# A four-layer transformer block on one core: the first norm and the last norm, taken tile by tile and moved to another engine

## The chip, the cores and the metric

The kernel runs on 1 core of one Trainium2 chip, in float32. The metric is the device time in microseconds; the median of three runs of the kernel before is 620.03 us (619.95 to 620.16). The core has five engines that run their own instruction streams in order: TensorE (PE in the profile, its weight loads PEld), VectorE (DVE), ScalarE (ACT), GpSimd (POOL) and SyncE (SP), which here only issues transfers.

## The reference, cut to what matters

```
x = h                                               # (2, 512, 256)
x = x + LN(attention(LN(x)))      # inside: its own LN with gain and bias, q/k/v for 16 heads of 128,
                                  # rotary embedding, causal softmax, output product, + its input
x = x + LN(ffn_nvfp4(LN(x)))      # gate, up, gelu, down; weights dequantised from 4-bit codes, 2048 wide
x = x + LN(linear_attention(LN(x)))   # running sums of k and k*v, q*kv / (q*k + eps), output product
x = x + LN(ffn_lut(LN(x)))        # gate, up, silu, down; weights looked up in a table of 16, 688 wide
```

LN takes mean and variance of each row of 256 and has no gain or bias of its own. The sums run in the order given, for 2 sequences of 512 rows.

## The kernel before

The 1024 rows are 8 tiles of 128 rows. A sequence has NT = 4 tiles; a unit is HT = 2 tiles (256 rows), and there are NUNIT = 4 units. Products need the contracted dimension on the partitions, so every normed tile is turned ("T" in a name: xT0 is the turned input of q, k and v, xT3 that of the last ffn).

The order of work is written out by hand. `slot(i)` (L1104) is one of the 32 heads: the scores of head i, the projections of q and k for head i + 1, the output product of head i - 2, the product of softmax and v of head i - 1, and the values of a later group of heads. pT, the softmax turned by VectorE and four transfers through SP, comes back one slot later. Pieces of work that wait for something (the norms, the linear attention, the last output) are generators, "chains"; PE's loops call `poll()` (L252), which resumes a chain when its planned time has come. The plan uses the estimated costs of `Engine.cost` (L111) and `Times`; only the order comes from it, and on the chip semaphores decide. Loads go through SP in program order.

The places that the change touches:

- **Start** (L297 to L301, L534 to L550): SP issues the four tiles of x, the columns of gains and biases, then wq, sin, wk, cos, the second halves of sin and cos, wv and so on. Nine warm-up matmuls (L554) run on PE on a tile of ones.
- **First norm** (`first_norms`, L580; its branch without wait from L685): for each of four tiles VectorE takes statistics and POOL takes a power for the factor rstd. For tiles 0 and 1 ACT writes mean - x into n (reading with a stride, `spread`, L627), then writes two diagonals -rstd, and PE multiplies n with the diagonal, which turns and scales in one product (L711). For tiles 2 and 3 VectorE writes (x - mean) * rstd and PE transposes (L725). ACT then applies gain and bias from PSUM to xT0, two tiles (256 columns) at a time (`affine`, L649). POOL and ACT copy xT0 into xTv, reordered for the values.
- **First q and k** (`projection`, L840): for head 0 in two halves of 256 columns. The first halves are started at L1226 to L1244. From L1243 on `halved` makes `matmul` (L276) split its stationary operand into two of 64 columns.
- **Norms between layers** (`norms`, L357): two statistics, x += y * rstd, two more statistics, n by ACT, VectorE transposes 32x32 blocks and SP sends four transfers (`by_blocks`, L386). Only for the last unit's third norm, PE transposes (L402) and ACT copies from PSUM, and `halved` is set back (L400).
- **Linear attention** (L1279), its output product po (L1350) and the last ffn: `silu_hidden` (L1373) in steps of two chunks o, `silu_out` (L1411), which makes two tiles one after the other, each accumulating six chunks in one of the two PSUM banks of tag "o", and `written` (L1429), which adds and stores.

Of the kernel before, what the change touches and what calls it, by code (L numbers as in the profile page):

```python
# [19 lines left out]
P = 128  # L20
# [3 lines left out]
D = 256  # L24
# [18 lines left out]
SWAPPED = (1, 2)  # L43
WARM = 9
REST = INTER - (NO - 1) * P
# [145 lines left out]
def sandwich_kernel(  # L191
    ctx: ExitStack,
    tc: tile.TileContext,
    x: bass.AP,
    wq: bass.AP,
    wk: bass.AP,
# [98 lines left out]


    x0 = [const.tile([P, NT, D], F32, name=f"x0_{b}") for b in range(B)]  # L297
    cols_sb = const.tile([P, 3 * NH + 2 * NK], F32, name="cols_sb")
    for t in range(NT):
        sync.dma_start(out=x0[0][:, t, :], in_=x[0][t * P : (t + 1) * P, :])  # L300
    sync.dma_start(out=cols_sb, in_=cols)  # L301
# [32 lines left out]
    def chunk(t, kc):  # L334

        return t[:, :, kc].rearrange("p a j t -> p j a t")
# [16 lines left out]
    def add_scaled(x, y, rstd):  # L353

        vector.scalar_tensor_tensor(x, y, rstd, x, ALU.mult, ALU.add)

    def norms(u, y, stage, to, eps=EPS, strided=False):  # L357

        x = [xs[u][:, j, :] for j in range(HT)]
        first = [stats(t, eps) for t in y]
        second = []
        for j in range(HT):
            yield until(first[j][0])
            add_scaled(x[j], y[j], first[j][0])
            second.append(stats(x[j], EPS))
        n = acts.tile([P, HT, D], F32, tag="ln", name=f"ln{stage}_{u}")


        by_blocks = (u, stage) != (NUNIT - 1, 3)
        for j in range(HT):
            rstd, shift = second[j]
            yield until(rstd, shift)
            to_n, from_x = n[:, j, :], x[j]
            if not by_blocks:
                to_n = to_n.rearrange("p (k f c) -> p k f c", k=NK, c=4)
                from_x = from_x.rearrange(
                    "p (c f k) -> p k f c" if strided else "p (k c f) -> p k f c", k=NK, c=4
                )  # L380
            elif strided:
# [4 lines left out]
        if by_blocks:  # L386

            tr = acts.tile([P, 4, NK, HT, 32], F32, tag="ln", name=f"tr{stage}_{u}")
            for j in range(HT):
                vector.transpose(  # L390
                    tr[:, :, :, j, :], n[:, j, :].rearrange("p (k c f) -> p c k f", k=NK, c=4)
                )
            for a in range(4):
                sync.dma_start(
                    out=to[:, a].rearrange("p k j t -> p (k j t)"),
                    in_=tr[32 * a : 32 * a + 32].rearrange("f c k j t -> f c (k j t)"),
                )
        else:

            halved[0] = False  # L400
            pt = bank("t")
            for kc in range(NK):  # L402
                for j in range(HT):
                    transpose(
                        pt[:, kc * TU + j * P : kc * TU + (j + 1) * P],
                        n[:, j, kc * P : (kc + 1) * P],
                    )
            for kc in range(NK):
                scalar.copy(
                    to[:, :, kc].rearrange("p a j t -> p j a t"),  # L410
                    pt[:, kc * TU : (kc + 1) * TU].rearrange("p (j a t) -> p j a t", j=HT, a=4),
                )
# [97 lines left out]
    with ExitStack() as at:  # L510
# [23 lines left out]
        first, second = slice(0, TU), slice(TU, S)  # L534
        load("q", 0, 0)
        sync.dma_start(out=sin_sb[:, first], in_=sin[:, first])
        load("k", 0, 0)
        sync.dma_start(out=cos_sb[:, first], in_=cos[:, first])
        sync.dma_start(out=sin_sb[:, second], in_=sin[:, second])
        sync.dma_start(out=cos_sb[:, second], in_=cos[:, second])  # L540
        load("v", 0)
        load("q", 0, 1)
        load("k", 0, 1)
# [36 lines left out]
        def first_norms(b, wait):  # L580
# [104 lines left out]
            else:  # L685
# [5 lines left out]
                def diagonal(t):  # L691
# [5 lines left out]
                    )  # L697

                for t in range(NT):
                    statistics(t)  # L700
                    variance(t)
                    if t < HT:
                        scalar.activation(*spread(t), AF.Identity, bias=mv[:, t, 0:1], scale=-1.0)
                    factor(t)
                for t in range(HT):
                    diagonal(t)

                quarters = [[bank(tag) for _ in range(NK)] for tag in "ts"]
                for t in range(HT):
                    for kc in range(NK):  # L710
                        matmul(  # L711
                            quarters[0][kc][:, t * P : (t + 1) * P],
                            n[0][:, t, kc * P : (kc + 1) * P],
                            wu[:, 0, (t + 1) * P : (t + 2) * P],
                            True,
                            True,
                        )
                centred(2)
                centred(3)
                for j in range(2):  # L720
                    if j:
                        yield 0.0
                        for kc in range(NK):
                            for t in (HT, HT + 1):
                                turn(quarters[1][kc][:, t % HT * P : (t % HT + 1) * P], kc, t)  # L725
                    for kc in range(NK):
                        affine(
                            scalar,
                            xT0[b][:, kc, j * TU : (j + 1) * TU],
                            quarters[j][kc][:, :TU],  # L730
                            kc,
                        )
            for kc in range(NK):
# [5 lines left out]
                )  # L739
            yield 30.0  # L740
            while holder[0] is not None:
# [98 lines left out]
        def projection(kind, i, tag="mm"):  # L840
# [9 lines left out]
            lo, hi = slice(0, 64), slice(64, 128)  # L850

            for cs in [slice(0, TU), slice(TU, S)] if i == 0 else [slice(0, S)]:
                ps = bank(tag)
                for kc in range(NK):
                    matmul(
                        ps[:, cs],
                        w[:, hh, kc, :],
                        chunk(xT0[b], kc) if b else xT0[b][:, kc, cs],
                        kc == 0,
                        kc == NK - 1,  # L860
                    )
                yield
                def by_scalar():
# [3 lines left out]

                first_half = i == 0 and cs.start == 0
                if i and (kind == "k") == (i > 1):
# [356 lines left out]
        pair = projection("q", 0), projection("k", 0, "o")  # L1226
        next(pair[0])
        begin(first, next(first))
        for rows, cs, base in (
            (slice(0, P), slice(S - P, S), 0),  # L1230
# [12 lines left out]
        halved[0] = True  # L1243
        next(pair[1])  # L1244
        for step in (*pair, *pair, *pair):
# [33 lines left out]
    def linear_attention(u):  # L1279
# [63 lines left out]
        for ch in range(NK):  # L1343
            for t in range(HT):
# [3 lines left out]
                yield 0.3  # L1348
        yield until(lT)
        po = bank("t" if last else "o")  # L1350
# [11 lines left out]

        yield from norms(u, [po[:, j * D : (j + 1) * D] for j in range(HT)], 3, t, 16 * EPS)
        xT3[u] = t
# [46 lines left out]
    def silu_out(u):  # L1411
        for t in range(HT):
            po = bank("o")[:, :D]
            last = (u, t) == (NUNIT - 1, HT - 1)
            for cs in [slice(0, P), slice(P, D)] if last else [slice(0, D)]:
                for o in range(NO):
                    matmul(
                        po[:, cs],
                        hT2[u % 2][:, o, t * P : (t + 1) * P],
                        wd[:, o, cs],  # L1420
                        o == 0,
                        o == NO - 1,
                    )
                    if o % 2 and (o + 1 < NO or cs.stop < D):
                        yield
            begin(written(u, t, po))
            yield

# [52 lines left out]
def _layout(i):  # L1481
# [21 lines left out]
    def turned(w):  # L1503
        return w.reshape(4, 32, -1).transpose(1, 0, 2).reshape(w.shape)

    def by_half(s):
        return s.reshape(4, 2, -1).transpose(1, 0, 2).reshape(s.shape)
# [12 lines left out]
    named = {  # L1520
        "x": i[a0 + "h"],
        "wq": by_head_chunk(i[a0 + "wq"]),
        "wk": by_head_chunk(i[a0 + "wk"]),
# [43 lines left out]
```

## Time and profile before

| | |
|---|---|
| median of 3 runs | 620.03 us |
| profiled execution | 620.06 us |
| its span | 618.1 us |
| PE busy | 611.0 us, 99% of the span |
| VectorE busy | 483.3 us, 78% |
| ACT busy | 312.0 us, 50% |
| POOL busy | 275.9 us, 45% |

The span is what the profile covers; the profiled execution took 1.96 us more than it. A line of a timeline is: start in us, length, engine, line of the code, operation, output<-inputs, shapes, count, and in brackets the idle time of the engine before it and what ended it. L183, L281 and L288 are lines of helpers that record every operation, so the names of the tiles tell which it is. PE is shown with 128*128 or 128*64, the size of its stationary operand; a float32 matmul leaves two records. "ps_mm", "ps_o", "ps_s" and "ps_t" are PSUM banks by tag, two of each. Lines with SPq are the issue of a transfer, not the transfer.

### The profile page before, as it was taken

How to read it: one execution, taken by the hardware profiler on the slowest of the kernel's cores; microseconds unless marked ns; L12 is line 12 of the kernel's file. 1: busy time of each engine (PE TensorE's matmuls, PEld its weight loads, DVE VectorE, ACT ScalarE, POOL GpSimd, SP SyncE). 2: the span in 40 equal slices, each digit the busy share in tenths (PEclk: the TensorE clock that was granted, in tenths of full speed). 3: DMA queues.
4: the chain of work that ended last, by engine and by line, in shares of the span. 5: the costliest groups of instructions: out<-in, count | busy, mean ns of one | idle time of the engine just before them, and what ended most of it. 6: DMA issues, size and time to landing. Idle time of an engine off the chain costs nothing.

```text
span 618.1 us, 13150 instructions
## 1 busy us (share of the span) xinstructions
PE 611.0 (99%) x4876; PEld 397.7 (64%) x4876; DVE 483.3 (78%) x1159; ACT 312.0 (50%) x717; POOL 275.9 (45%) x353
## 2 busy tenths in 40 slices
PE   8999999999999999999999999999999999999996
PEld 6555655555555555656667788888666666666676
DVE  6989989887887999989899989779985463384853
ACT  5657776776666657667566741234123313425130
POOL 5355656454553575755667300440360160163341
PEclk9999999999999999999999999999999999999999
DMA  8467474755547547556543521310000001001000
GB/s 227 137 168 211 107 198 125 173 165 147 155 125 182 164 113 190 156 143 173 124 130 63 131 57 24 113 35 18 1 20 19 1 1 35 1 5 31 27 27 18
DMA packets 43599, 60.90 MB, mean 99 GB/s; under 512 B 5136, under 2 KB 31504, under 8 KB 43536
## 3 DMA queue, kind: packets, MB, share of 16 engines
q1 hardware_dynamic: 43536, 60.07, 37.5%
q8 instruction: 39, 0.64, 0.4%
q14 instruction: 24, 0.20, 0.1%
HBM read 28.33 MB, written 1.05 MB: 48 GB/s over the span
## 4 chain that ended last, share of the span: by engine, by line
PE 96%; DVE 2%; issue 1%; DMA 0%; POOL 0%; ACT 0%; POOLq 0%; DVEq 0%
PE ps_mm L281 39%; PE ps_o L281 22%; PE ps_s L281 21%; PE ps_t L281 14%; DVE rr L183 0%; DMA x<-in_x 0%; DVE turned L183 0%; DVE st L183 0%; DVE wu L183 0%; DVE xTv L183 0%; DVE xT L183 0%; DVE ra L183 0%; DVE hT L183 0%; POOLq L1563 0%; PE ps_t L288 0%
## 5 line engine op out<-in xcount | busy, mean ns | idle before, releaser
L183 DVE SCALAR_TENSOR_TENSOR rr<-ps_mm,cols_sb,sin_sb 64x512 f32<-64x512 f32 (+1 forms) x126 | 93.4, 741 | 3.7 <-PE ps_mm L281 0.8
L183 POOL TENSOR_TENSOR wg<-wg,scratch 128x752 f32<-128x752 f32 x30 | 53.8, 1794 | 91.0 <-DVE scratch L183 88.7
L281 PE MATMUL ps_mm<-xT,wg 128*64 128x256 f32 (+2 forms) x680 | 85.8, 379 | 0.0
L183 ACT ACTIVATE p<-p,mn 128x512 f32<-128x512 f32 (+3 forms) x128 | 70.3, 551 | 28.1 <-DVE mn L183 27.9
L281 PE MATMUL ps_s<-xT,wu 128*64 128x256 f32 (+1 forms) x652 | 82.0, 379 | 0.0
L281 PE MATMUL ps_o<-wd,hT 128*64 128x256 f32 (+2 forms) x676 | 78.3, 375 | 0.0
L281 PE MATMUL ps_t<-pT,v 128*64 128x256 f32 (+3 forms) x512 | 75.1, 433 | 0.0
L281 PEld LDWEIGHTS ps_mm<-xT,wg 128*64 128x64 f32 (+2 forms) x680 | 56.5, 139 | 19.1 <-ACT ge L183 0.3
L281 PEld LDWEIGHTS ps_o<-wd,hT 128*64 128x64 f32 (+1 forms) x676 | 55.5, 141 | 20.7
L183 ACT ACTIVATE p<-p,rs 128x512 f32<-128x512 f32 (+3 forms) x128 | 61.4, 551 | 11.4 <-DVE rs L183 9.8
L281 PEld LDWEIGHTS ps_s<-xT,wu 128*64 128x64 f32 (+1 forms) x652 | 54.4, 139 | 18.1 <-DVE hT L183 0.3
L281 PEld LDWEIGHTS ps_t<-pT,v 128*64 128x64 f32 x512 | 42.0, 137 | 34.8 <-issue 25.5
L281 PE MATMUL ps_o<-wo,oT 128*64 128x256 f32 x512 | 61.4, 379 | 0.0
L281 PE MATMUL ps_mm<-xT,wq 128*64 128x512 f32 (+2 forms) x252 | 59.4, 582 | 0.4 <-ACT xT L183 0.4
L281 PE MATMUL ps_mm<-xT,wk 128*64 128x512 f32 x248 | 59.1, 592 | 0.0
L281 PEld LDWEIGHTS ps_o<-wo,oT 128*64 128x64 f32 x512 | 42.5, 137 | 25.2 <-issue 15.1
L183 POOL TENSOR_TENSOR ra<-ra,cos_sb 128x512 f32<-128x512 f32 (+1 forms) x33 | 41.1, 1246 | 39.3 <-ACT ra L183 37.1
L281 PE MATMUL ps_s<-kT,qT 128*64 128x64 f32 (+5 forms) x384 | 57.4, 425 | 0.1
L183 DVE STREAM_TRANSPOSE turned<-p 128x512 f32<-128x512 f32 (+3 forms) x128 | 54.1, 479 | 2.1 <-DMA pT<-turned 0.6
L281 PE MATMUL ps_mm<-wv,xTv 128*64 128x256 f32 x464 | 55.6, 379 | 0.0
L183 DVE TENSOR_TENSOR hT<-ge,ps_s 128x512 f32<-128x512 f32 x32 | 21.8, 684 | 41.6 <-ACT ge L183 22.9
L281 PEld LDWEIGHTS ps_s<-kT,qT 128*64 128x64 f32 x384 | 34.3, 137 | 24.2 <-issue 7.5
(157 smaller groups left out, 933.6 us busy)
## 6 DMA issues: line engine op xcount, KB each, us to landing
pT<-turned SPq DMA_DIRECT2D x128, 208.0 KB, 3.9
wo<-in_wo SPq DMA_DIRECT2D x17, 256.0 KB, 4.1
wv<-in_wv SPq DMA_DIRECT2D x16, 256.0 KB, 4.0
wq<-in_wq SPq DMA_DIRECT2D x15, 256.0 KB, 4.4
wk<-in_wk SPq DMA_DIRECT2D x15, 256.0 KB, 4.0
xT<-tr SPq DMA_DIRECT2D x44, 64.0 KB, 2.1
pk_g<-in_gate_p SPq DMA_DIRECT2D x4, 256.0 KB, 4.3
sc_g<-in_gate_s SPq DMA_DIRECT2D x8, 128.0 KB, 4.1
```

What stands on the lines that cost most here:

```text
L183: return write(*args, **more)
L281: nc.tensor.matmul(out[part], lhsT=lhsT[:, part], rhs=rhs, start=start, stop=stop, **more)
```

## The change

At the start:

- the host hands in tiles 0 and 1 of the first sequence with their columns reordered (`x_turned`), so ACT reads them contiguously; the true rows are loaded into the same place later, 20 planned us after the norm;
- tiles 0 to 3 are centred, turned and given gain and bias one by one, each with its own affine of 128 columns; of tile 1 VectorE makes one of the two;
- the first half of q is made tile by tile, and the products of q and k stand between the turns of tiles 2 and 3;
- wk is loaded ahead of sin, and the first half of cos behind wv; there are eight warm-up matmuls instead of nine.

At the end, for the last unit:

- its third norm is done like the others (VectorE transposes, transfers), but VectorE makes n as well as the sum for rstd (`last_norms`); PE transposes nothing, and `halved` stays set;
- the output product of its linear attention is planned 0.8 us earlier;
- the output product of the unit before (`silu_out(2)`) accumulates four chunks of both tiles, then the last two of both.

In the instruction lists of the two programs, all engines have the same order between the start and the last unit, but for the two reloads on SP, which stand behind the transfers of the second head's pT and ahead of the next loads of wk, wv, wo and of the gate's codes and scales. At the end, PE has the eight halved matmuls of the linear attention's output product four instructions earlier; VectorE has the add x<-ps_o of unit 1's second output tile behind the last three hT products of unit 2, where it stood ahead of two of them; ACT has the two x<-x,shift ahead of the last two si.

```
-WARM = 9
+WARM = 8
...
+        src = x_turned if t < HT else x[0]
+        sync.dma_start(out=x0[0][:, t, :], in_=src[t * P : (t + 1) * P, :])
...
+    def last_norms(u, y, to, eps):
+        x = [xs[u][:, j, :] for j in range(HT)]
+        def factors(y, eps):
...
+            vector.bn_stats(st, y)
+            vector.bn_aggr(mv, st)
+            vector.tensor_scalar(ve, mv[:, 1:2], eps, None, ALU.add)
+            pool.tensor_tensor(rstd, ve, mhalf[:, :1], ALU.pow)
+            return mv, rstd
+        first = [factors(t, eps) for t in y]
+        second = []
+        for j in range(HT):
+            add_scaled(x[j], y[j], first[j][1])
+            second.append(factors(x[j], EPS))
+        yield 2.3
...
+        for j in range(HT):
+            mv, rstd = second[j]
+            vector.tensor_scalar(n[:, j, :], x[j], mv[:, 0:1], rstd, ALU.subtract, ALU.mult)
+            turned_about(tr, n, j)
+        brought(to, tr)
+        yield 1.0
+        for j in range(HT):
+            mv, rstd = first[j]
+            pool.tensor_scalar(shift, mv[:, 0:1], rstd, -1.0, ALU.mult, ALU.mult)
+            scalar.activation(x[j], x[j], AF.Identity, bias=shift)
+        yield until(to)
...
         load("q", 0, 0)
+        load("k", 0, 0)
         sync.dma_start(out=sin_sb[:, first], in_=sin[:, first])
-        load("k", 0, 0)
-        sync.dma_start(out=cos_sb[:, first], in_=cos[:, first])
         sync.dma_start(out=sin_sb[:, second], in_=sin[:, second])
         sync.dma_start(out=cos_sb[:, second], in_=cos[:, second])
         load("v", 0)
+        sync.dma_start(out=cos_sb[:, first], in_=cos[:, first])
...
+                def centred_rows(t):
+                    scalar.activation(
+                        n[0][:, t, :], x0[b][:, t, :], AF.Identity, bias=mv[:, t, 0:1], scale=-1.0
+                    )
                 for t in range(NT):
                     statistics(t)
                     variance(t)
-                    if t < HT:
-                        scalar.activation(*spread(t), AF.Identity, bias=mv[:, t, 0:1], scale=-1.0)
+                    if t == 0:
+                        centred_rows(0)
                     factor(t)
+                diagonal(0)
+                centred_rows(1)
+                diagonal(1)
+                def turned_to(engines, t, pts):
+                    for kc in range(NK):
+                        affine(engines[kc], xT0[b][:, kc, t * P : (t + 1) * P], pts[kc], kc)
+                firsts = []
+                for t, tag in ((0, "t"), (1, "s")):
+                    firsts.append([bank(tag)[:, :P] for _ in range(NK)])
...
                 centred(2)
+                turned_to([scalar, scalar], 0, firsts[0])
+                turned_to([vector, scalar], 1, firsts[1])
                 centred(3)
+                pts = [bank("t") for _ in range(NK)]
+                for t in (2, 3):
+                    yield 0.0
                     for kc in range(NK):
+                        turn(pts[kc][:, (t - 2) * P : (t - 1) * P], kc, t)
+                    turned_to([scalar, scalar], t, [p[:, (t - 2) * P : (t - 1) * P] for p in pts])
...
-            yield 30.0
+            yield 20.0
+            if b == 0:
+                for t in range(HT):
+                    sync.dma_start(out=x0[b][:, t, :], in_=x_rows[b][t * P : (t + 1) * P, :])
+            yield 10.0
...
+                first_half = i == 0 and cs.start == 0
+                tiles = [slice(0, P), slice(P, TU)] if first_half and kind == "q" else [cs]
+                for n, (ts, kc) in enumerate((ts, kc) for ts in tiles for kc in range(NK)):
...
+                    if first_half and (kind, n) in (("q", 1), ("k", 0)):
+                        yield
...
         next(pair[0])
+        next(first)
+        next(pair[0])
+        next(pair[1])
         begin(first, next(first))
+        next(pair[1])
...
-        yield until(lT)
+        yield until(lT) - 0.8 * last
...
+        if u == NUNIT - 2:
+            parts = [(t, slice(0, D), os) for os in (range(NO - 2), range(NO - 2, NO)) for t in range(HT)]
+        else:
+            parts = [(0, slice(0, D), range(NO))]
+            parts += [(1, cs, range(NO)) for cs in (halves if u == NUNIT - 1 else [slice(0, D)])]
+        po = {}
+        for n, (t, cs, os) in enumerate(parts):
+            if t not in po:
+                po[t] = bank("o")[:, :D]
...
+    def turned_columns(x):
+        return x.reshape(-1, NK, 4, 32).transpose(0, 1, 3, 2).reshape(x.shape)
```

`turned_about` and `brought` are the VectorE transpose and the four transfers that `norms` had in its by_blocks branch.

More of the change, by code (lines that the diff above doesn't have):

```diff
@@ L194, in sandwich_kernel @@
     x: bass.AP,
+    x_turned: bass.AP,
     wq: bass.AP,
@@ L294, in until @@
         return max(0.0, times.written(*aps) - now[0])
+    x_rows = x
     x0 = [const.tile([P, NT, D], F32, name=f"x0_{b}") for b in range(B)]
@@ L299, in sandwich_kernel @@
     for t in range(NT):
-        sync.dma_start(out=x0[0][:, t, :], in_=x[0][t * P : (t + 1) * P, :])
+        src = x_turned if t < HT else x[0]
+        sync.dma_start(out=x0[0][:, t, :], in_=src[t * P : (t + 1) * P, :])
     sync.dma_start(out=cols_sb, in_=cols)
@@ L355, in add_scaled, with turning, turned_about, brought @@
         vector.scalar_tensor_tensor(x, y, rstd, x, ALU.mult, ALU.add)
+    def turning(u, stage):
+        return acts.tile([P, 4, NK, HT, 32], F32, tag="ln", name=f"tr{stage}_{u}")
+    def turned_about(tr, n, j):
+        vector.transpose(tr[:, :, :, j, :], n[:, j, :].rearrange("p (k c f) -> p c k f", k=NK, c=4))
+    def brought(to, tr):
+        for a in range(4):
+            sync.dma_start(
+                out=to[:, a].rearrange("p k j t -> p (k j t)"),
+                in_=tr[32 * a : 32 * a + 32].rearrange("f c k j t -> f c (k j t)"),
+            )
+    def last_norms(u, y, to, eps):
+        x = [xs[u][:, j, :] for j in range(HT)]
+        def factors(y, eps):
+            st = small.tile([P, 6], F32, tag="st", name="st")
+            mv = small.tile([P, 2], F32, tag="mv", name="mv")
+            vector.bn_stats(st, y)
+            vector.bn_aggr(mv, st)
+            ve = small.tile([P, 1], F32, tag="ve", name="ve")
+            vector.tensor_scalar(ve, mv[:, 1:2], eps, None, ALU.add)
+            rstd = small.tile([P, 1], F32, tag="rstd", name="rstd")
+            pool.tensor_tensor(rstd, ve, mhalf[:, :1], ALU.pow)
[6 more added lines that the diff above has]
+        yield 2.3
+        n = acts.tile([P, HT, D], F32, tag="ln", name=f"n_{u}")
+        tr = turning(u, 3)
+        for j in range(HT):
[6 more added lines that the diff above has]
+            mv, rstd = first[j]
+            shift = small.tile([P, 1], F32, tag="shift", name="shift")
+            pool.tensor_scalar(shift, mv[:, 0:1], rstd, -1.0, ALU.mult, ALU.mult)
+            scalar.activation(x[j], x[j], AF.Identity, bias=shift)
+        yield until(to)
     def norms(u, y, stage, to, eps=EPS, strided=False):
@@ L368, in norms @@
         n = acts.tile([P, HT, D], F32, tag="ln", name=f"ln{stage}_{u}")
-        by_blocks = (u, stage) != (NUNIT - 1, 3)
         for j in range(HT):
@@ L375, in norms @@
             to_n, from_x = n[:, j, :], x[j]
[L376 to L381, printed above, removed]
+            if strided:
                 to_n = to_n.rearrange("p (k m) -> p k m", k=NK)
@@ L385, in norms @@
         yield until(n)
[L386 to L412, printed above, removed]
+        tr = turning(u, stage)
+        for j in range(HT):
+            turned_about(tr, n, j)
+        brought(to, tr)
         for j in range(HT):
@@ L697, in diagonal @@
                     )
+                def centred_rows(t):
+                    scalar.activation(
+                        n[0][:, t, :], x0[b][:, t, :], AF.Identity, bias=mv[:, t, 0:1], scale=-1.0
+                    )
                 for t in range(NT):
@@ L701, in first_norms @@
                     variance(t)
-                    if t < HT:
-                        scalar.activation(*spread(t), AF.Identity, bias=mv[:, t, 0:1], scale=-1.0)
+                    if t == 0:
+                        centred_rows(0)
                     factor(t)
[L705 to L709, printed above, removed]
+                diagonal(0)
[7 more added lines that the diff above has]
+                    firsts.append([bank(tag)[:, :P] for _ in range(NK)])
                     for kc in range(NK):
                         matmul(
-                            quarters[0][kc][:, t * P : (t + 1) * P],
+                            firsts[t][kc],
                             n[0][:, t, kc * P : (kc + 1) * P],
@@ L718, in first_norms @@
                 centred(2)
+                turned_to([scalar, scalar], 0, firsts[0])
+                turned_to([vector, scalar], 1, firsts[1])
                 centred(3)
[L720 to L725, printed above, removed]
-                    for kc in range(NK):
[L727 to L732, printed above, removed]
+                pts = [bank("t") for _ in range(NK)]
+                for t in (2, 3):
+                    yield 0.0
+                    for kc in range(NK):
+                        turn(pts[kc][:, (t - 2) * P : (t - 1) * P], kc, t)
+                    turned_to([scalar, scalar], t, [p[:, (t - 2) * P : (t - 1) * P] for p in pts])
             for kc in range(NK):
@@ L853, in projection @@
                 ps = bank(tag)
-                for kc in range(NK):
+                first_half = i == 0 and cs.start == 0
+                tiles = [slice(0, P), slice(P, TU)] if first_half and kind == "q" else [cs]
+                for n, (ts, kc) in enumerate((ts, kc) for ts in tiles for kc in range(NK)):
                     matmul(
-                        ps[:, cs],
+                        ps[:, ts],
                         w[:, hh, kc, :],
-                        chunk(xT0[b], kc) if b else xT0[b][:, kc, cs],
+                        chunk(xT0[b], kc) if b else xT0[b][:, kc, ts],
                         kc == 0,
@@ L865, in by_scalar @@
                     pool.tensor_mul(a[:, cs], a[:, cs], cos_sb[:, cs])
-                first_half = i == 0 and cs.start == 0
                 if i and (kind == "k") == (i > 1):
@@ L1243, in sandwich_kernel @@
         halved[0] = True
-        next(pair[1])
         for step in (*pair, *pair, *pair):
@@ L1361, in linear_attention @@
         t = gp.tile(TURNED, F32, tag="xT3", name=f"xT3_{u}", bufs=4)
-        yield from norms(u, [po[:, j * D : (j + 1) * D] for j in range(HT)], 3, t, 16 * EPS)
+        y = [po[:, j * D : (j + 1) * D] for j in range(HT)]
+        yield from last_norms(u, y, t, 16 * EPS) if last else norms(u, y, 3, t, 16 * EPS)
         xT3[u] = t
@@ L1411, in silu_out @@
     def silu_out(u):
[L1412 to L1427, printed above, removed]
+        halves = [slice(0, P), slice(P, D)]
+        if u == NUNIT - 2:
[7 more added lines that the diff above has]
+                po[t] = bank("o")[:, :D]
+            for o in os:
+                matmul(
+                    po[t][:, cs],
+                    hT2[u % 2][:, o, t * P : (t + 1) * P],
+                    wd[:, o, cs],
+                    o == 0,
+                    o == NO - 1,
+                )
+                if o % 2 and (o + 1 < NO or cs.stop < D):
+                    yield
+            if o == NO - 1 and cs.stop == D:
+                begin(written(u, t, po[t]))
+                yield
     def written(u, j, y):
@@ L1521, in _layout @@
         "x": i[a0 + "h"],
+        "x_turned": turned_columns(i[a0 + "h"][0, : HT * P]),
         "wq": by_head_chunk(i[a0 + "wq"]),
```

## The prediction

> **What bounds the kernel now.** I read the page's busy line, then the chain that ended last, then the chain in order of time around the two places that the change touches, then the timeline there for what runs beside.
>
> ```profile
> PE 611.0 (99%) x4876; PEld 397.7 (64%) x4876; DVE 483.3 (78%) x1159; ACT 312.0 (50%) x717; POOL 275.9 (45%) x353
> PE 96%; DVE 2%; issue 1%; DMA 0%; POOL 0%; ACT 0%; POOLq 0%; DVEq 0%
> ```
>
> TensorE (PE) is 96% of the chain. From 8.06 us to the last matmul the chain has no piece of another engine, so time is won only by starting that unbroken stretch earlier or by taking PE work out of it. The pieces in the head, and in the tail:
>
> ```profile
> 5.32 0.95 PE ps_t L281 x6
> 6.27 0.03 issue
> 6.29 0.57 ACT xT L183
> 6.87 0.04 issue
> 6.91 1.16 PE ps_mm L281 x4
> 8.06 0.44 PE ps_s L288 x4
> 8.50 1.01 PE ps_o L281 x8
> 9.52 0.86 PE ps_mm L281 x8
> ...
> 592.66 1.73 PE ps_o L281 x16
> 594.39 0.59 PE ps_t L288 x4
> 594.97 3.46 PE ps_o L281 x16
> ```
>
> Columns: start, length, what. In the head PE alternates with ACT until 6.91; from there it is packed: first half of q (ps_mm), turn of tiles 2 and 3 (ps_s L288), first half of k (ps_o), second half of q at 9.52. In the tail four transposes take 0.59 between two groups of the last-but-one output product. Full-width and halved matmuls cost the same: the 8 halved records at 591.80 take 0.86 us and the 4 full ones at 598.43 take 0.86. So leaving the tail halved (line 400 is gone) is free, and I cost it at 0 (bounds -0.1 and +0.1 for the last product with 128 columns, whose 24 full records go at 0.11 each).
>
> **The head.** The timeline's rows for ACT and for the wait behind the second tile:
>
> ```profile
> 3.51 1.47 ACT L183 ACTIVATE n<-x,mv 128x256 f32<-128x256 f32 x2 [1.09 <-DVE mv L183]
> 4.88 0.68 ACT L183 ACTIVATE wu<-wu,rstd 128x128 f32<-128x128 f32 x2
> 6.29 1.02 ACT L183 ACTIVATE xT<-ps_t,cols_sb 128x256 f32<-128x256 f32 x2 [0.73 <-PE ps_t L281]
> ```
>
> ACT centres both tiles, then builds both diagonals, then both 256-wide affines. Now it goes tile by tile. Working forward with these durations:
>
> 1. Centring reads contiguously (x is turned on the host). Strided it took 0.74; the contiguous 256-wide ACTIVATE (p<-p,rs) takes 0.49, with some 0.4 to the next start. It starts at 3.51 as before; rstd of tile 0 is ready at 3.75+0.56=4.31, so diagonal 0 runs 4.34 to 4.72 (0.38). Tile 1's centring follows at 4.63, its diagonal (rstd at 4.48+0.55=5.03) 5.07 to 5.45.
> 2. PE turns tile 0 from 4.78 (was 5.32). A first 128-column record ends 0.38 after its start, each further one 0.11 later: 5.26 for the first half of the columns, 5.49 for the second; tile 1 ends 5.99 and 6.22.
> 3. The affines are 128 wide: 0.56 less 0.13 (the step between 256 and 128 columns at about 1 ns each) is 0.43. ACT does tile 0 at 5.36 and 5.69 (ends 6.13). VectorE's piece of tile 1 stands between n(2), which ends at 5.80+0.53=6.33, and n(3) at 6.78, where VectorE waited 0.45 for POOL anyway; at 0.35 (the 256-wide one from PSUM takes 0.48) it ends at 6.70 and costs nothing there.
> 4. PE: q of tile 0 ends at 6.7, tile 2's transposes at 6.9, q of tile 1 waits for 6.70 and ends at 7.46, k's first half-product 7.89, tile 3's transposes 8.11, k's second 8.54.
> 5. ACT's affines of tile 3 run 8.04 to 8.47 and 8.37 to 8.80. So the second half of q starts at 8.52; its first pair is out at 8.95, where before it was 9.35+0.38=9.73. **PE's stretch starts 0.78 us earlier.**
>
> What is late next: the scores start at 14.52 now, so at 13.74. They need kT and qT. VectorE's chain from the second half of q to kT is 10.58 to 14.36, 3.78 us; from 9.64 it ends at 13.42. POOL's qT (12.30 to 13.56 now) follows xTv, the three mask selects and two multiplies, which start 0.4 earlier, and ends near 13.2. Both are covered, by 0.3 and 0.5; if that cover is gone the gain falls by the difference. Transfers: wk and sin change places, and the first cos goes behind wv. By the transfer view the early 128 KB loads land 2.1 (x) to 4.4 us (the second wk) after issue, wv after up to 5.1. wk, issued at 3.52 and 3.0 in flight before, is needed at 7.4; cos, issued at 5.89, lands by 10.3 at the latest and POOL wants it near 10.4. The values need wv near 10.1; issued at 5.42 (now 5.89) it lands by 10.5 at the latest, which would cost up to 0.4.
>
> Removing one of nine warm-up matmuls takes nothing off the path: the last one starts at 4.40, real work at 5.32. The two reloads of x's tiles, issued on SP behind the second head's pT, cost SP two issues of about 0.6 (the row of xT<-tr); behind them stand six loads and the next pT. SP stood idle from 40.1 to 42.45 there, so 1.2 fits; the bandwidth for 256 KB (about 0.9 us at 290 GB/s) could push a pT against its product. Bounds 0 to 0.3 lost; I take 0. From there the instruction lists of the two programs are the same up to the last unit, so the shift is carried to the tail. Head: 0.78, bounds 0.4 (wv late, or POOL and VectorE end last) and 1.1 (no restart cost at any of PE's new waits).
>
> The warm-up rows show records 0.213 apart (9 records starting 1.78, 2.13 us in all), and 0.11 apart at the end (6 starting 3.70, 0.97 in all): PE runs at half rate until about 3.8, 2.8 us after the first. [...]
>
> **The tail.** The transposes on PE go: 0.59. In their place VectorE makes n, transposes it and SP sends four transfers. Working on the clock of before: the output product of the linear attention moves ahead of four matmuls and ends 0.86 earlier, 584.89. VectorE: two statistics, two adds, two more statistics at 0.43+0.18+0.15 and 0.49 each, the first output tile's two operations and the second's statistics, then n twice (about 0.4) and two transposes (0.43): to about 591.95. Four issues of 0.6 and 2.1 to landing make 596.0; PE wants xT at 597.8. So the transfer is hidden, by 1.8.
>
> But a new wait replaces the transposes. The last-but-one output product now accumulates both tiles side by side, so its second tile needs the other ps_o bank 1.7 us after the first, at 594.2. That bank is freed by VectorE's add x<-ps_o of the unit before, which stood at 590.79 and now is queued behind n, the transposes and all three hT products. The last hT cannot be earlier:
>
> ```profile
> 590.79 0.48 DVE L183 SCALAR_TENSOR_TENSOR x<-ps_o,rstd,x 128x256 f32<-128x256 f32 x1
> 592.79 0.64 ACT L183 ACTIVATE si<-ps_mm 128x256 f32<-128x256 f32 x2
> 593.66 0.42 DVE L183 TENSOR_TENSOR hT<-si,ps_mm 48x256 f32<-48x256 f32 x1
> ```
>
> It waits for si, which waits for PE's matmul that ends at 592.65. ACT has the two x<-x,shift ahead of si now; their shifts stand on POOL behind the second output tile's ve, rstd and shift, which take 1.32 after its statistics (596.52 to 597.84 in a later row), so they come at 590.46+1.32+2x0.26=592.3. So si starts near 592.9, hT ends at 594.2, the add at 594.68. PE starts then, first pair out at 594.73+0.43=595.16; unhindered it would be 594.60. Stall 0.56 of the 0.59. At best (si at 592.74) the add ends at 594.53 and the stall is 0.4; with VectorE's chain 0.3 later it is 0.85. **Tail: -0.03, bounds -0.2 and +0.3.**
>
> **Sum.** 620.06 (profiled execution; span 618.1 and 1.96 around it) - 0.78 - 0.03 = 619.25. The median of before is 620.03, 0.03 lower, so 619.2.
>
> **Rivals.**
> - *More is won*, 618.6: PE restarts cost less than 0.1 each and the head gives 1.1 to 1.2, with the tail at its best end of 0.2. For it: the weight loads run ahead of the matmuls (PEld 64%). Against: n(2) at 6.33 and VectorE's piece at 6.70 are fixed by POOL's rstd.
> - *The head's gain is lost*, 620.0: wv lands late, qT or kT ends last, or a pT lands behind the reloads, and the tail stalls 0.85. For it: cover of only 0.3 to 0.5. Against: SP's idle time and the unchanged order.
> - *Slower*, 621.6: eight warm-ups leave PE at half rate when the real work starts at 4.8. Until the second half of q, 20 records of 128 columns and 4 of 256 (28 units) would cost 0.1 more each, 2.8, of which about 0.5 falls in waits: 619.25+2.3. It decides only if full rate is not there by about 4.8; before, it came near 3.8, inside the eight.
> - *The change does not do what it says*: the tail is that case in part, as its PE time is given back as a wait.
>
> **Numbers.** Within 0.2% (1.24 us, about what a measurement here can tell from no change) lies 618.79 to 621.27. Forecast 0.63, more won 0.17, gain lost 0.14, slower 0.06. So faster 0.17, same 0.77, slower 0.06. Range: head 0.4 to 1.1, middle 0 to 0.3 lost, tail +0.2 to -0.3: 618.7 to 620.3, drawn to 618.5 for part of the second case.
>
> **What would show it.** Right: PE's second half of q near 8.5, the scores near 13.7, no transposes at the tail, and a wait of PE on VectorE (x<-ps_o) of about half a microsecond before the second tile of the last-but-one output product. Wrong: warm-up records still 0.21 apart at their end, PE waiting on a transfer (wv, cos, xT), or no wait in the tail.

## The result and the profile after

The changed kernel takes 619.11 us by median (618.87 to 619.63, 18 runs), the kernel before beside it 620.16 us (619.91 to 620.95, 18 runs). The ratio is 0.9984, 95% interval 0.9977 to 0.999: 1.05 us less, 0.16%, which is inside the 0.2% that count as no change here. The profiled execution took 618.87 us with a span of 617.1 (before: 620.06 and 618.1).

The page's busy line and its shares of the chain, after:

```profile
PE 610.6 (99%) x4966; PEld 413.4 (67%) x4966; DVE 485.4 (79%) x1168; ACT 309.7 (50%) x716; POOL 276.2 (45%) x347
PE 95%; DVE 3%; issue 1%; DMA 0%; POOL 0%; ACT 0%; POOLq 0%; DVEq 0%; ACTq 0%
```

PE has 0.4 us less to do, and VectorE's share of the chain has risen from 2% to 3%. The chain in order of time shows where. In the head (columns: start, length, what):

```profile
4.86 0.80 PE ps_t L282 x4
5.66 0.64 PE ps_s L282 x4
6.30 0.52 PE ps_mm L282 x4
6.82 0.22 PE ps_t L289 x2
7.04 0.45 PE ps_mm L282 x4
...
8.59 1.07 PE ps_mm L282 x8
9.66 0.86 PE ps_o L282 x8
```

The reader is to see that the chain now stays on PE from 4.86 on until the tail, with no piece of ACT between its products (before, ACT's xT stood at 6.29 and PE was packed from 6.91). The second half of q, x8 at 8.59, is to be compared by the timeline's starts, 8.58 against 9.35: the chain's 9.52 of before is only where the piece ahead of it ends. In the tail, the end of the same chain:

```profile
593.28 0.49 DVE x L183
593.77 0.14 issue
593.91 3.67 PE ps_o L282 x32
597.58 0.86 PE ps_mm L282 x8
```

The four transposes are gone, and in their place the chain leaves PE: the second tile of the last-but-one output product waits until VectorE's add x frees its bank. The list of PE's waits names it, the only one besides the wait for the first memset:

```profile
PE ps_o L581 <- POOL mhalf L183: 1.0, 1, 1.0
PE ps_o L282 <- DVE x L183: 0.5, 1, 0.5
```

To compare executions whose first transfer lands at different moments, I measured stretches between starts of PE records (and of VectorE's first statistic) in all twelve profiles. Columns: A from the first statistic to the values (ps_t<-wv); B from the values to the first scores; C from the first product of pT and v to the twenty-first; D from the first hidden product of the last-but-one unit to that of the last unit, which holds the tail's change; then the median, and the ratio to before with its interval (before was run again beside each of them, with medians of 620.16 to 620.20).

| run | A | B | C | D | median us | ratio (95%) |
|---|---|---|---|---|---|---|
| before | 8.24 | 3.45 | 216.46 | 11.82 | 620.16 | |
| after | 7.46 | 3.56 | 216.18 | 11.91 | 619.11 | 0.9984 (0.9977 to 0.9990) |
| e1 head only | 7.46 | 3.57 | 216.43 | 11.82 | 619.32 | 0.9986 (0.9977 to 0.9995) |
| e2 tail only | 8.31 | 3.44 | 216.20 | 11.90 | 619.82 | 0.9996 (0.9987 to 1.0004) |
| e3 in turn | 7.46 | 3.56 | 216.19 | 11.22 | 618.34 | 0.9971 (0.9960 to 0.9983) |
| e4 add early | 7.46 | 3.55 | 216.34 | 11.22 | 618.38 | 0.9972 (0.9961 to 0.9983) |
| e5 nine warm-ups | 7.46 | 3.55 | 216.78 | 11.90 | 619.18 | 0.9982 (0.9973 to 0.9991) |
| e6 four warm-ups | 8.66 | 3.56 | 216.19 | 11.91 | 620.52 | 1.0006 (0.9997 to 1.0015) |
| e7 strided | 7.96 | 3.57 | 216.19 | 11.90 | 619.20 | 0.9985 (0.9976 to 0.9994) |
| e8 old order | 7.68 | 3.57 | 216.18 | 11.91 | 618.92 | 0.9981 (0.9972 to 0.9990) |
| e9 contiguous only | 8.21 | 3.44 | 216.27 | 11.83 | 619.89 | 0.9995 (0.9986 to 1.0004) |
| e10 strided, in turn | 7.60 | 3.55 | 216.19 | 11.23 | 618.31 | 0.9970 (0.9959 to 0.9981) |

### The profile page after: what moved, and what is told of

Read it like the earlier page. It is cut to its first block, busy times and chain, and to the rows that moved or that the text cites. A ratio compares the mean times of both kernels' runs of the same rounds, so it can differ in the third digit from the quotient of the medians.

```text
span 617.1 us, 13345 instructions
## 1 busy us (share of the span) xinstructions
PE 610.6 (99%) x4966; PEld 413.4 (67%) x4966; DVE 485.4 (79%) x1168; ACT 309.7 (50%) x716; POOL 276.2 (45%) x347
## 3 DMA queue, kind: packets, MB, share of 16 engines
HBM read 28.59 MB, written 1.05 MB: 48 GB/s over the span
## 4 chain that ended last, share of the span: by engine, by line
PE 95%; DVE 3%; issue 1%; DMA 0%; POOL 0%; ACT 0%; POOLq 0%; DVEq 0%; ACTq 0%
PE ps_mm L282 39%; PE ps_o L282 21%; PE ps_s L282 20%; PE ps_t L282 14%; DVE st L183 0%; DVE x L183 0%; DVE rr L183 0%; DMA x<-in_x_turned 0%; DVE hT L183 0%; DVE turned L183 0%; DVE mv L183 0%; DVE wu L183 0%; POOL rstd L183 0%; DVE xTv L183 0%; DVE xT L183 0%
## 5 line engine op out<-in xcount | busy, mean ns | idle before, releaser
L282 PE MATMUL ps_mm<-xT,wg 128*64 128x256 f32 x704 | 86.1, 379 | 0.0
L282 PE MATMUL ps_s<-xT,wu 128*64 128x256 f32 x672 | 82.2, 379 | 0.0
L282 PE MATMUL ps_o<-wd,hT 128*64 128x256 f32 (+1 forms) x728 | 78.3, 372 | 0.5 <-DVE x L183 0.5
L282 PEld LDWEIGHTS ps_o<-wd,hT 128*64 128x64 f32 x728 | 54.9, 137 | 22.1 <-issue 0.9
L282 PEld LDWEIGHTS ps_mm<-xT,wg 128*64 128x64 f32 x704 | 56.2, 137 | 19.5 <-ACT ge L183 0.3
L282 PEld LDWEIGHTS ps_t<-pT,v 128*64 128x64 f32 x512 | 47.3, 137 | 29.5 <-issue 21.0
L282 PEld LDWEIGHTS ps_s<-xT,wu 128*64 128x64 f32 x672 | 54.2, 137 | 18.4 <-DVE hT L183 0.3
L282 PEld LDWEIGHTS ps_o<-wo,oT 128*64 128x64 f32 x512 | 46.9, 137 | 20.7 <-issue 14.0
L282 PE MATMUL ps_s<-kT,qT 128*64 128x448 f32 (+5 forms) x384 | 57.4, 425 | 0.1
```

What stands on the lines that cost most here:

```text
L282: nc.tensor.matmul(out[part], lhsT=lhsT[:, part], rhs=rhs, start=start, stop=stop, **more)
```

## The experiments

**e1, the head alone.** Before, with the first norm, q and k, loads and warm-ups of the change, and the old norms, linear attention and last output product.

> The head of the change on the kernel before; the tail is the old one, with its four transposes. My theory (head 0.72 us won, as the traces of before and after show at the values, 11.24 against 10.52; middle nothing; tail about nothing): 0.7 us faster than before, 0.6 to 0.8 by medians, a span of 617.2 to 617.4, no wait of PE in the last unit. Rival A, that the tail was worth the 0.3 us by which the two profiled executions differ beyond the head (1.19 in all): 0.7 here too, but about 0.3 in e2. Rival B, that these 0.3 us were won in the middle by the head (the reloads, the transfers' new order): 1.0 us faster. Rival C, chance: in the profile of before one head's pT landed at 170.32, 5.8 us after its last issue, where most take 4.0 to 4.7, and PE waited 0.2 for it; then here too the middle shifts by at most that 0.2 in one head, differently from run to run.

Measured: 619.32 us, 0.85 less than before. A is 7.46, as in after, D is 11.82, as in before, and C is 216.43, as in before. So the 0.28 by which after's profile is shorter in C is not the head's doing: rival B falls. Rival C holds in kind, though the shift can be larger than its 0.2 (0.54 at one head in e5). The profiled execution of before shows the cause in one head, in the timeline's row of the weight loads (in brackets: idle time before, and what ended it):

```profile
170.36 0.20 PEld L281 LDWEIGHTS ps_t<-pT,v 128*64 128x64 f32 x4 [0.46 <-DMA pT<-turned]
```

The last packet of that pT landed at 170.32, 5.8 us after its last issue. Over the twelve profiles C is 216.18 to 216.20 in seven and longer by 0.08 to 0.60 in five (before, e1, e4, e5, e9). In before, e1 and e5 the step lies at this same head, the fourteenth, whose last pT lands 4.5 to 6.0 us after its issue in the twelve (4.5 is the median of all heads); in e4 it lies at the third, where no late transfer was looked for. In e5, whose C is the longest, PE's list of waits shows it:

```profile
PE ps_t L282 <- DMA pT<-turned: 0.3, 1, 0.3
```

So a late pT is an event of an execution, with the change and without it (e5 differs from after by one warm-up only). What makes this head's transfer late was not tried.

**e2, the tail alone.** Before, with the last unit's norms by VectorE, the earlier output product of the linear attention, the interleaved output product and the halved tail.

> The tail of the change on the kernel before (nine warm-ups, the old head). My theory: the transposes' 0.59 us are given back by the wait for the ps_o bank; in after, the shift against before goes from 0.98 us ahead of the last-but-one unit's hidden product to 0.87 behind its output product, so the tail loses 0.1 there and wins 0.05 to 0.15 at the end (halved last product). Time within 0.15 us of before. Rival A (the tail wins the 0.3 that the head does not explain): 0.3 us faster. A wait of PE on VectorE's x of 0.4 to 0.6 us ahead of the second tile of the last-but-one output product in either case. In the middle nothing that differs from before but a single late pT.

Measured: 619.82 us, ratio 0.9996 (0.9987 to 1.0004), so no difference is shown, and by the times alone rival A's 0.3 is not excluded either. The trace is sharper here: D goes from 11.82 to 11.90, 0.08 lost, with a wait of PE on x of 0.5, as in after. Rival A's 0.3 would have to be somewhere in the trace; the stretches behind D (to the last unit's output product 9.50 against 9.49, and from there to the last add 7.04 against 7.07) give back 0.02 in all. So the work of the tail is worth nothing. Behind the last add the span ends 3.10 us later against 3.29 in before; that is not the tail's work either, as the part on the tail below shows.

**e3, the last-but-one output product in turn.** After, with one condition changed, so that the two tiles are made one after the other again:

```
-        if u == NUNIT - 2:
+        if u < 0:
             parts = [(t, slice(0, D), os) for os in (range(NO - 2), range(NO - 2, NO)) for t in range(HT)]
```

> After, with the last-but-one unit's output product tile by tile again (all six chunks of one tile, then of the other). Then the second ps_o bank is needed 2.6 us after the first product starts instead of 1.73, that is at 594.1 by after's clock, and VectorE's add frees it at 593.76. My theory: the wait (0.67 us between PE's records at 593.24 and 593.91) goes whole and nothing takes its place, since the two last hT chunks (592.79 and 593.25) are wanted at 593.24 and 593.67: 0.6 to 0.7 us faster than after, about 1.7 us faster than before. Rival: PE then waits for hT (the order that the change gave up was bad for that reason): the fifth chunk's semaphore comes some 0.1 late, so only 0.4 to 0.5 is won. Second rival: the next unit's xT is then late: it lands near 595, wanted at 596.7: no.

Measured: 618.34 us, 0.77 less than after and 1.83 less than before. D is 11.22: 0.69 less than in after, 0.60 less than in before, which is the transposes' 0.59. The chain has PE alone again in that place:

```profile
590.82 0.86 PE ps_mm L282 x8
591.68 5.18 PE ps_o L282 x48
596.86 0.86 PE ps_mm L282 x8
```

All 48 records of both tiles run without a gap, where after had 3.67 us of them behind a wait. Neither hT nor xT takes the wait's place: xT's last transfer landed at 595.01, 1.7 us ahead of its first use.

**e4, the add moved up.** After, with the add of the second unit's second tile planned one unit of time earlier; on VectorE it then stands ahead of the last two hT products, and PE's order is that of after:

```
-            yield until(rstd, shift)
+            yield until(rstd, shift) - 1.0 * ((u, j) == (1, 1))
             add_scaled(x, y, rstd)
```

> After, with the add x<-ps_o of the second unit's second tile (and the shift behind it) moved on VectorE ahead of the last two hT products, into the 0.82 us in which VectorE waits for si. The order of PE is that of after. My theory (the wait is for the bank that this add frees): the bank is free at about 592.1, the wait goes whole: 0.6 to 0.7 us faster than after, the same as e3 within 0.1. Rival (the wait is for something else that comes at the same time, hT or si): the wait stays, as in after, or grows by the 0.5 by which the hT products are pushed back.

Measured: 618.38 us, D 11.22, both as e3. VectorE's timeline, where the add (ps_o,rstd,x) fills the time in which VectorE waited for ACT's si:

```profile
590.91 0.65 DVE L183 TENSOR_TENSOR hT<-si,ps_s 128x512 f32<-128x512 f32 x1
591.48 0.47 DVE L183 SCALAR_TENSOR_TENSOR x<-ps_o,rstd,x 128x256 f32<-128x256 f32 x1
592.05 0.35 DVE L183 TENSOR_SCALAR x<-x,shift 128x256 f32<-128x256 f32 x1
592.38 0.42 DVE L183 TENSOR_TENSOR hT<-si,ps_s 128x256 f32<-128x256 f32 x1
592.83 0.42 DVE L183 TENSOR_TENSOR hT<-si,ps_mm 48x256 f32<-48x256 f32 x1
```

The hT products end at 593.25, as in after, although the add now stands ahead of them. So PE waited for the bank that the add frees, and for nothing else: the rival (hT or si) would have left the wait. Two different cures, a later need and an earlier release, take it away whole.

**e5, nine warm-ups.** `WARM = 9` in after.

> After with nine warm-up matmuls instead of eight. In the six profiles so far PE's records come 0.11 apart (full rate) from 3.91 in two, not before the last warm-up (4.34) in three, and in one not before 4.77; in after the first record of the real work, at 4.86, took 0.46 and the next came 0.30 behind it, where 0.21 is usual. Eighteen records of 0.213 from 0.98 end at 4.82 at the latest, so a ninth takes no time from the first turn at 4.76 to 4.86. Theory A (eight are enough; full rate comes by the time since PE started, whatever runs): within 0.15 us of after, about 1.05 us faster than before. Theory B (in part of the executions eight leave PE at half rate for some of the real work): the median falls below that of after by 0.1 to 0.4, and the spread of the single times is smaller.

Measured: 619.18 us against 619.11, A 7.46 in both: theory A by its numbers. Its premise, that the time since PE started is what counts, falls with e6. The single times spread by 0.63 us against 0.76, too near to support theory B.

**e6, four warm-ups.** `WARM = 4` in after.

> After with four warm-ups: eight records that end near 2.7, and then 2.1 us in which PE is idle. Theory A (full rate comes by the time since PE started, whatever it did since): full rate by 4.9 as with eight, same time as after. Theory B (it takes some 3 to 4 us of work without a long gap): the first turn, q's first half and the first chunks of k run at half rate, records 0.21 apart, until 7.7 or later; 16 records of 128 columns and 4 of 256 at 0.1 and 0.2 more each are 2.4 us, of which some lie in waits for ScalarE's affines: 1.0 to 2.4 us slower than after, so about 0 to 1.4 us slower than before. This is the size that the prediction's slower rival would have.

Measured: 620.52 us, 1.4 more than after; A is 8.66, 1.20 more. PE's timeline:

```profile
4.75 1.22 PE L282 MATMUL ps_t<-wu,n 128*128 128x128 f32 x4 [1.70 <-ACT wu L183]
5.77 1.06 PE L282 MATMUL ps_s<-wu,n 128*128 128x128 f32 x4
6.62 1.06 PE L282 MATMUL ps_mm<-xT,wq 128*128 128x128 f32 x4
7.47 0.64 PE L289 MATMUL ps_t<-ident,n 128*128 128x128 f32 x2
7.90 0.68 PE L282 MATMUL ps_mm<-xT,wq 128*128 128x128 f32 x4
```

Behind the first, groups of four records take 1.06 until 7.5, and 0.68 at 7.90, where the records' spacing falls from 0.213 to 0.11: 3.2 us after the work resumed at 4.75. Theory B by its size: four warm-ups with a pause of 1.7 us behind them cost 1.4 us against eight.

**e7, strided.** After without the turned copy of x:

```
-        src = x_turned if t < HT else x[0]
+        src = x[0]
...
-                    scalar.activation(
-                        n[0][:, t, :], x0[b][:, t, :], AF.Identity, bias=mv[:, t, 0:1], scale=-1.0
-                    )
+                    scalar.activation(*spread(t), AF.Identity, bias=mv[:, t, 0:1], scale=-1.0)
...
-            if b == 0:
-                for t in range(HT):
-                    sync.dma_start(out=x0[b][:, t, :], in_=x_rows[b][t * P : (t + 1) * P, :])
```

> After without the turned copy of x: all four tiles are loaded as they are, ScalarE's centring of tiles 0 and 1 reads in strides again (0.74 us each, contiguous 0.50), and the two reloads on SP go. Theory: tile 0's centring (3.57 to 4.31) still ends before its diagonal can start (4.41, rstd), so it costs nothing; tile 1's ends 0.25 later, and with it ScalarE's next rows: diagonal 1 and the affines of tile 0 (5.47 to 5.72): q's first half starts 0.2 to 0.25 later, and the scores 0.2 later. So 0.2 us slower than after in the head, and nothing won in the middle by the reloads that are gone: 0.85 us faster than before. Rival (the reloads cost something): the middle is 0.1 to 0.3 faster than in after, so that the time is that of after.

Measured: 619.20 us, 0.1 more than after. C is 216.19 without the reloads and 216.18 with them, the same, so the reloads cost nothing that shows. A is 7.96, 0.50 more than in after, twice what the strides should cost. PE's timeline tells why:

```profile
4.78 1.22 PE L282 MATMUL ps_t<-wu,n 128*128 128x128 f32 x4
5.79 1.00 PE L282 MATMUL ps_s<-wu,n 128*128 128x128 f32 x4
6.63 0.61 PE L282 MATMUL ps_mm<-xT,wq 128*128 128x128 f32 x4
```

The first turn takes 1.22, as in e6 and not 0.71 to 0.80: PE was still at half rate, until about 6.5, though it had eight warm-ups and a pause of only 0.2 us. This run could not say what the strides cost; e10 was made for that.

**e8, the old order of loads.** After, with sin ahead of k's weights and the first half of cos ahead of the second half of sin.

> After with the early loads in the order of before: sin ahead of k's weights, the first half of cos behind them, ahead of sin's second half. Theory: k's weights then land near 6.9 (in after 5.84) and PE wants them at 7.32; v's land near 9.9 (8.89), wanted at 10.35; so the order is worth nothing by itself, the time is that of after within 0.15. Rival: PE waits for wk or wv by 0.1 to 0.5, with a wait on that transfer in the profile, and the time is so much longer.

Measured: 618.92 us, 0.2 less than after, with intervals that overlap. PE waits for no weight. By the medians the order is worth nothing by itself. Its A is 0.22 longer than after's: there ACT's second diagonal waited for rstd, because x's second tile, whose place in the order is the same in both, landed 2.52 us after its issue instead of 2.28. That this is chance, and not the order, was not tried in a second profile.

**e9, the contiguous read alone.** Before, with the turned copy, the contiguous centring and the reloads (the edit is the reverse of e7's, on the old code by pairs of tiles).

> Before, with only the turned copy of x: tiles 0 and 1 are loaded turned and centred with contiguous reads (0.50 instead of 0.74), and reloaded later; the work still goes by pairs of tiles, with nine warm-ups and the old order of loads and the old tail. Theory (the two halves of the head's change add up): the first diagonal waits for rstd (4.31) and is ready near 4.7, the second (rstd at 5.03) at 5.45 instead of 5.56; so PE's first turn starts near 4.8 but its second tile ends only 0.1 to 0.25 earlier than before, and the wide affines, q's first half and the scores come 0.1 to 0.25 earlier: 0.1 to 0.25 us faster than before. Going tile by tile is then worth the rest of the 0.72, 0.45 to 0.6. Rival (the contiguous read is the main thing): the scores come at 14.0, 0.5 us or more earlier.

Measured: 619.89 us, ratio 0.9995 (0.9986 to 1.0004). A is 8.21, 0.03 less than before. The first turn began 0.19 earlier (5.13) and lost that again, its first record 0.38 ahead of the next where 0.21 is usual, as PE came to full rate only near 5.5. So it is inconclusive on the size between 0 and 0.25. The trace speaks against the rival's 0.5: even with the 0.17 that the clock took (0.38 less 0.21), the gain would be 0.20, and the scores start at 14.51 and not at 14.0. The interval of the times alone, down to 0.9986, would still hold 0.5.

**e10, strided and in turn.** e3 and e7 together.

> The version of e3 (last-but-one unit's output product tile by tile) without the turned copy of x, so without the reloads: e7 and e3 together. In e7's profile PE had full rate only from 6.4 us, and its first turn, at 4.77, ran with records 0.21 apart; so what the strides cost could not be told from what the clock cost there. Theory A (the clock's onset falls differently in each execution, whatever the kernel; the strides cost 0.1 to 0.25): by medians 0.1 to 0.25 us slower than e3, some 1.6 us faster than before; and in a profile in which full rate is there by 4.9, the scores start 0.1 to 0.25 later than e3's 13.85. Theory B (e7's late onset belongs to the kernel): full rate late here too, scores near 14.3, 0.45 us slower than e3.

Measured: 618.31 us, 1.89 less than before, the least of all, and no different from e3 (618.34). In this execution PE came to full rate in its last warm-up, ahead of the real work:

```profile
4.75 0.71 PE L282 MATMUL ps_t<-wu,n 128*128 128x128 f32 x4
5.67 0.71 PE L282 MATMUL ps_s<-wu,n 128*128 128x128 f32 x4 [0.21 <-ACT wu L183]
```

The only trace of the strides is the 0.21 for which PE waits for the second diagonal, and A is 7.60, 0.14 more than in e3: theory A. In the time these 0.14 do not show. Theory B falls: with e7's head, the late onset did not come again.

## Why the prediction was right, and where its steps failed

**The head** was forecast at 0.78 and is 0.78 in A (8.24 to 7.46), in five of the six runs with eight or nine warm-ups, the turned copy and the new code (the sixth is e8, with its late tile). On the page's clock it reads 0.72 at the values (11.24 to 10.52), because x's first tile landed 2.15 us after its issue in after and 2.08 in before; over the twelve profiles it takes 2.00 to 2.17. Within it, going tile by tile is worth 0.64 (e10 against before: 8.24 to 7.60) and the contiguous read 0.14 (e10 against e3); the order of loads (by the medians of e8) and the reloads are worth nothing, as forecast.

**The cover of kT** was sized wrong, and failed. The prediction had kT end at 13.42, 0.3 ahead of the scores, with VectorE's old duration of 0.69. The rows of before, then VectorE's and PE's rows in after:

```profile
12.30 1.26 POOL L183 TENSOR_TENSOR qT<-ra,rr 128x512 f32<-128x512 f32 x1
13.67 0.69 DVE L183 TENSOR_TENSOR kT<-ra,rr 128x512 f32<-128x512 f32 x1
...
11.95 1.27 POOL L183 TENSOR_TENSOR qT<-ra,rr 128x512 f32<-128x512 f32 x1
12.81 0.96 DVE L183 TENSOR_TENSOR kT<-ra,rr 128x512 f32<-128x512 f32 x1
13.88 0.23 PEld L282 LDWEIGHTS ps_s<-kT,qT 128*64 128x64 f32 x4 [0.80 <-POOL qT L183]
```

The profile puts the wait to POOL's qT, but that had ended at 13.22; kT ended at 13.77 and is what came last. It took 0.96, with POOL's qT beside its first 0.4 us; in before it began after qT had ended (13.67 against 13.56) and took 0.69. It is so in all twelve profiles: 0.94 to 0.98 in the nine where the two overlap by some 0.4, and 0.69 in before, e2 and e9, where they do not. That POOL slows VectorE is read from this agreement; no run moved qT alone. So the scores start 0.11 later than PE could (B, 3.45 to 3.56). That costs nothing in the end: before lost the same 0.11 at the second head's scores, 1.84 for the ten records that take 1.73 in after.

**The warm-up** is the step that was right in its number and wrong in its reason. The prediction read one profile, put full rate near 3.8 (by its single records it is 4.0, since the first of the six records at 3.70 is still at half rate), and held the slower rival to be decided by that, "inside the eight". Over the profiles with eight or nine warm-ups full rate, records 0.11 us apart instead of 0.213, comes between 4.0 (before, e3) and 6.5 (e7). It came behind the start of the real work with eight (after and e7, and by less than 0.1 in e4 and e8) and with nine (e2, e9). A ninth makes no difference to the time (e5). So the slower rival does occur, in part of the executions, but at a price of 0 to 0.4 and not 2.3: in after the first turn took 0.80 instead of 0.71 and A is still 7.46, since VectorE's and ACT's rows held PE up later anyway; in e7 it cost 0.36 beyond the strides. Even e6, with half rate until 7.9, lost 1.20. What sets the moment was not shown: with eight or nine warm-ups it comes 3.0 to 5.5 us after PE's first record, and in e6 3.2 us after the work resumed behind the pause of 1.7.

**The middle** was forecast at nothing, and C says so. The 0.28 by which the two first profiles differ there is the late pT of before. The profiled executions differ by 1.19 us in all: the head on the page's clock is 0.72, C 0.27 before rounding, the tail -0.08 by D and what follows, the end behind the last add 0.12, and 0.18 lies outside the span (1.95 against 1.77; 1.77 to 2.15 in the twelve). These make 1.21; the other stretches and rounding take 0.02.

**The tail** was forecast to win 0.03; it loses 0.09 in D, 0.03 of it given back behind up to the last add. The mechanism was right in every step: the bank, the add behind n, the transposes and the three hT products, the late si, the hidden transfer (xT's last part landed at 595.03). The stall was sized at 0.56 and is 0.67 (591.51 + 1.73 = 593.24 to 593.91): si started at 591.98 and hT ended at 593.25, so the add came at 593.28 as forecast for its place in the order (the prediction's 594.2 less the 0.98 by which after is ahead), but PE started 0.14 after the add's end, where the prediction took 0.05.

Behind the last add the span ends 3.29 us later in before and 3.17 in after, and these 0.12 bring the whole tail near its forecast by luck, for the prediction has no such term. In all twelve traces the last write takes 1.34 to 1.35 us from its issue to its last packet. What differs is how many of SP's closing semaphore waits, some 0.06 us each, stand behind the wait for that write: four in before, three in e1 and e9, two in after, one in e2, e7 and e10, where the span ends 1.42, 1.39, 1.31 and 1.25 us behind that packet.

So the forecast of 619.2 was near 619.11 for reasons that mostly hold: 0.78 won in the head, and a tail that takes a wait for the work it removes. By the two profiles the gain is 0.84 (0.78, less 0.06, and the 0.12 of the end); the median's 1.05 agrees with that within its interval (0.6 to 1.4).

## What to carry to other kernels

When PE work is removed by handing it to another engine, look at what that engine's queue held before: here a bank's release was pushed behind the new work, and the saved 0.59 us came back as a 0.67 us wait, until one line moved either the need or the release. Differences of a few tenths between two profiles should be traced stretch by stretch before they are credited to an edit; a late transfer, the moment of full rate and the first load's landing each move a single execution by as much. And a margin read from one execution (a transfer's, the clock's) is one draw from a spread.

## What the runs showed of the hardware that I had not expected

- With eight or nine warm-ups, PE's records come 0.213 us apart for the first 3.0 to 5.5 us from the first record, and 0.11 apart after that. The moment differs between executions of the same head: in e3 it falls inside the sixteen records of the warm-ups, at 4.0, in after behind them all, at 5.1. Half rate in the first records of the real work cost up to 0.4 us with eight or nine warm-ups (e7), and 1.2 with four.
- The same VectorE product (kT, 128x512) took 0.69 us in before and 0.96 in after, where POOL's product of the same shape runs beside its first 0.4 us; the second head's, which VectorE also makes, took 0.66 in all twelve, 2 us or more behind the end of POOL's.
- The pT transfers, four of 208 KB, land 4.5 us after the last issue by median, but up to 6.0 in single heads, and in the fourteenth head PE's room for them goes from 1.2 us down to a wait of 0.5.
- What an execution takes outside the span varies by 0.4 us (1.77 to 2.15).
